# The activation of VectorE's channels, moved half a slot down in ScalarE's order (patch-matching denoiser, 8 images, one core)

## The chip, the cores and the metric

The kernel runs on one core of a Trainium2 chip. The core has TensorE (PE, matrix products), VectorE (DVE, elementwise work), ScalarE (ACT, activations and copies), GpSimd (POOL, here mostly an issuer of DMAs) and SyncE (SP, an issuer of DMAs). The metric is the device time in microseconds of the whole program. The profile is of one execution; all times in the views count from the start of its span.

## The reference

The input x has 8 images of 32 channels and 128 x 128 pixels, float32. Layer 0 normalises it by groups of channels (`_gn`), finds for each pixel the 8 of 25 neighbours in a 5 x 5 window whose 3 x 3 patches are nearest, and gathers them into 256 channels. These channels pass three stages, each a 1 x 1 convolution (256 to 256 channels) followed by a depthwise 3 x 3 convolution and an activation, and a final part:

```
dct = _conv(xb, dct_w, groups=C)
h = jax.nn.relu(_conv(_conv(xb, w1), w2, groups=CK, pad=1))
h = jax.nn.relu(_conv(_conv(h, w3), w4, groups=CK, pad=1))
wiener = jax.nn.sigmoid(_conv(_conv(h, w5), w6, groups=CK, pad=1))
filt = _conv(wiener * dct, inv_dct_w, groups=C)
return _conv(filt, agg_w)
```

x plus that result goes to layer 1, which normalises again and adds one 5 x 5 convolution per channel.

## The kernel before

An image is cut into strips of 8 rows, 16 and one partial strip per image, so 136 steps (`steps`) for 8 images; two more drain the pipeline. The main loop runs over steps, and inside a step over four slots, `for i in (3, 2, 1, 0)`: the slot of stage 3, of stage 2, of stage 1, and of the final part (0). Stage i works in step s on strip s - (i - 1), the final part on strip s - 2. So the result of stage 1 is read by stage 2 in the next step's slot 2, that of stage 2 by stage 3 in the next step's slot 3, and that of stage 3 by the final part in slot 0 of the step after: three slots after the one in which it was begun, each time.

The 256 channels are two halves of 128. For one half the depthwise convolution runs on TensorE (`depthwise_t`, tile pw, L751, activated out of PSUM by L764). For the other half it runs on VectorE (`depthwise_v`): the 1 x 1 convolution's result pv (L670) is copied to tile tv by ScalarE (L678, two copies), ScalarE writes the first tap into acc (L722), VectorE adds eight taps (L725, some 10.5 us), ScalarE applies the activation in place (L729), and SP copies two rows of tv for the next strip (`rows_before_v`, L655). The 1 x 1 convolution for the TensorE half is p (L694), copied to tile t by ScalarE (L701, two copies) and shifted between partitions by SP's DMAs (L707, L709, L648). Where the 1 x 1 convolution sums over both halves, pv takes four matmuls from acc[0], TensorE's half, and then four from acc[1], VectorE's half, and this twice (rows 0 to 3 and 4 to 7).

Beside the stages each slot selects and gathers one unit of neighbours for a later strip: a DMA by POOL brings indices (ib, L602), ScalarE turns them into one-hot selections (L616 and L617, twice a slot: `gather_select(..., (0,))` early and `(1,)` late), TensorE multiplies (pg, L631, 48 records) and ScalarE copies the result (L638). The next image's preparation (squared differences L444 and L452, sums pd L459, the choice of neighbours L536 and L537, transpositions), layer 1 (L897, L924, L936) and the final part (pc L810, the products L818, pa L831, L839) fill in from queues "D", "A", "P" and "Q" or at fixed places.

PE, DVE and ACT run in the order in which the program writes their instructions (`tc.manual_schedule`); the order of DMA issues on POOL and SP is set when the program is built. Generators hold back pieces of a stage for a later slot. `depthwise_v` writes L722 up to its first yield, the taps up to its second, the activation up to its third and then the row copy. In the main loop `new_v` is the generator begun in this slot, `dv` that of the slot before and `kept` that of the slot before that. `next(dv)` therefore writes the activation late in the slot after the taps, behind the queue "A" and ahead of the second selection, and `next(kept)` writes the row copy in the middle of the slot after that, behind `pointwise_t` and ahead of `gather_pixels`. The taps of stage 3 thus have their activation late in slot 2, those of stage 2 late in slot 1, those of stage 1 late in slot 0.

Of the kernel before, what the change touches and what calls it, by code (L numbers as in the profile page):

```python
# [44 lines left out]
def bm3d_conv_preact(  # L45
# [165 lines left out]
    def push(task):  # L211
        want = next(task, None)
        if want:
            which, cost, *wait = want
            queues[which].append((cost, task, now[0] + (wait[0] if wait else 0)))
# [54 lines left out]
    def weights():  # L270

        natural, kc = {}, None
        for i, (name, w) in enumerate((("w1", w1), ("w3", w3), ("w5", w5))):
            t = accp.tile([P, 2, R * W // 2], F32, name=f"nat_{name}", tag=f"acc{i + 1}0")
            natural[name] = t = t[:, :, :CK]
            nc.sync.dma_start(t, w.rearrange("(m p) i a b -> p m (i a b)", p=P))
        yield "D", 1.0, 8

        nat = natural["w1"]
        kc = accp.tile([P, 2, R * W // 2], F32, name="w1_kc", tag="acc31")  # L280
        natural["w1"] = kc = kc[:, :, :CK]
        for m in range(2):
            for g in range(2):
                nc.vector.tensor_copy(
                    kc[:, m, P * g : P * (g + 1)].rearrange("p (j c) -> p j c", c=C),
                    nat[:, m].rearrange("p (c j g) -> p g j c", j=4, g=2)[:, g],
                )
        for name, dst in (("w1", lw1), ("w3", lw3), ("w5", lw5)):
            for g in range(2):
                yield "P", 0  # L290
                ps = ps_x.tile([P, 512], F32, name=f"ps_{name}_{g}", tag="x")
                for m in range(2):
                    nc.tensor.transpose(
                        ps[:, m * P : (m + 1) * P],
                        natural[name][:, m, g * P : (g + 1) * P],
                        ident,
                    )
                nc.scalar.copy(dst[:, g], ps[:, :CK])
# [67 lines left out]
    def prep(b):  # L366

        xn = load_image(b, nc.gpsimd) if b else first
        yield "P", 0
        yield "D", 5.5  # L370
        st = work.tile([P, 8, 6], F32, name=f"st_{b}", tag="st")
        for i in range(8):
            nc.vector.bn_stats(
                st[:, i], xn[:, 3 + 4 * i : 7 + 4 * i, 2 : 2 + W]
            )
        mv = work.tile([P, 2], F32, name=f"mv_{b}", tag="mv")
        nc.vector.bn_aggr(mv, st.rearrange("p a b -> p (a b)"))
        yield "A", 0
        nc.scalar.copy(xn[:, :, 0:2], xn[:, :, 2:3].to_broadcast([P, HR, 2]))
        nc.scalar.copy(  # L380
            xn[:, :, 2 + W :], xn[:, :, 1 + W : 2 + W].to_broadcast([P, HR, 2])
        )
        mr = yield from group_stats(mv, f"a{b}")
        nc.vector.tensor_scalar(
            xn, xn, mr[:, 0:1], mr[:, 1:2], op0=ALU.subtract, op1=ALU.mult
        )
        push(sources(b, xn))

        idx = work.tile([P, 4, 8, K, 4], U32, name=f"idx_{b}", tag="idx", bufs=1)

        sq = dram.tile([NO // 2, 4, HR - 2, HX], F32, name=f"sq_{b}", tag="sq")
        for i in range((HR - 2) // SR):
            pd = ps_d.tile([P, SR // 2, HX], F32, name=f"pd_{b}_{i}", tag="pd")

            for aa in ((2, 4), (0, 0), (1, 1), (3, 2), (4, 3), (5, 5)):
                yield "D", PAIR
                push(squares(b, i, pd, xn, aa, sq, idx))
# [254 lines left out]
    def rows_before_v(i, b, n):  # L652
        v = tv[i - 1]
        if n < NS:
            nc.sync.dma_start(v[:, 0:2], v[:, R : R + 2])  # L655
        else:
            nc.gpsimd.memset(v[:, 0 : i + 1], 0.0)
# [53 lines left out]
    def depthwise_v(i, b, n):  # L711
        v = tv[i - 1]
        nr = R if n < NS else i
        out_ = accp.tile([P, R, W], F32, name=f"acc{i}_{b}_{n}_1", tag=f"acc{i}1")
        acc = out_[:, :nr]
        for k, (dy, dx) in enumerate(
            ((1, 1), (0, 0), (0, 1), (0, 2), (1, 0), (1, 2), (2, 0), (2, 1), (2, 2))
        ):
            tap = dwv[:, i - 1, 3 * dy + dx : 3 * dy + dx + 1]
            rows = v[:, dy : dy + nr, dx : dx + W]  # L720
            if k == 0:
                nc.scalar.activation(acc, rows, AF.Copy, scale=tap)  # L722
                yield out_
            else:
                nc.vector.scalar_tensor_tensor(  # L725
                    acc, rows, tap, acc, op0=ALU.mult, op1=ALU.add
                )
        yield
        nc.scalar.activation(acc, acc, funcs[i - 1])  # L729
        yield  # L730
        rows_before_v(i, b, n)

    def depthwise_t(i, b, n):
# [297 lines left out]
    def until(cond, credit):  # L1031
        while not cond():
            turn(credit)

    with tc.manual_schedule(engines=ORDERED):
        push(prep(0))
        push(weights())
        push(mixes())
        xbd[0] = dram.tile([P, 2, H, W], F32, name="xbd_0", tag="xbd")
        for i in range(3):  # L1040
            nc.gpsimd.memset(tb[i][0:64, 0], 0.0)
        for u in range(7):
            unit(gather_load, u)

            for _ in range({2: 3, 3: 1}.get(u, 0)):
                turn(4.0)
            unit(gather_select, u - 2)
            unit(gather_pixels, u - 3)
        u = 4

        dt = dv = kept = iter(())

        later = iter(())

        for s in range(len(steps) + 2):
            if s < len(steps):
                b, n = steps[s]
                if s == 2:
                    push(bands())
                if n == (0 if b else 4) and b + 1 < NB:  # L1060
                    until(lambda: b in ready, 4.0)
                    push(prep(b + 1))
                if n == NS - 1 and b + 1 < NB:
                    until(lambda: b + 1 in ready, 4.0)
                    xbd[b + 1] = dram.tile([P, 2, H, W], F32, name=f"xbd_{b+1}", tag="xbd")
            for i in (3, 2, 1, 0):
                si = s - (i - 1 if i else 2)
                live = 0 <= si < len(steps)
                new_v = new_t = iter(())
                if live:  # L1070
                    bi, ni = steps[si]

                if live and i:
                    src = source(i, bi, ni)
                    pointwise_v(i, bi, ni, lws[i - 1], src)
                    new_v, new_t = depthwise_v(i, bi, ni), depthwise_t(i, bi, ni)
                    accs[i, bi, ni] = [None, next(new_v)]
                next(later, None)
                if live and not i:
                    if ni == 0:  # L1080
                        x1d[bi] = dram.tile([C, H, W], F32, name=f"x1d_{bi}", tag="x1d")
                        stats[bi] = work.tile([P, NS + 1, 6], F32, name=f"stat_{bi}", tag="stat")
                    xr, xf, j0, j1 = fins.pop(si)
                run("P")
                if live and not i:
                    final_dct(bi, ni, accs[3, bi, ni], xf, j0, j1)

                run("Q")
                if s < len(steps):
                    unit(gather_select, u + 1, (0,))  # L1090
                    unit(gather_load, u + 3)
                    tick(b, i)
                next(later, None)
                next(new_v, None)
                if live and i:
                    pointwise_t(i, bi, ni, lws[i - 1], src)
                next(kept, None)
                if s < len(steps):
                    unit(gather_pixels, u)
                next(dt, None)  # L1100
                run("A")
                next(dv, None)
                if s < len(steps):
                    unit(gather_select, u + 1, (1,))
                    u += 1
                next(dt, None)
                kept, dv, dt = dv, new_v, new_t
                if live and not i:
                    later = end(bi, ni, xr, j0, j1)
                if not i and 0 <= s - 1 < len(steps):  # L1110
                    fins[s - 1] = final_load(*steps[s - 1])
        next(kept, None)
        for _ in later:
            pass
        until(lambda: {(NB - 1, 0), (NB - 1, 1)} <= done, 4.0)
# [62 lines left out]
```

## Time and profile before

| what | us |
|---|---|
| median of three runs (lowest, highest) | 6544.47 (6539.76, 6554.23) |
| the profiled execution's own time | 6544.27 |
| its span, first to last instruction | 6542.5 |
| granted TensorE clock, mean over the span | 0.98 |
| L725, VectorE's taps: busy, mean of one | 4032.1, 1.237 |
| L729, the activation: 408 times, busy, mean of one | 417.3, 1.023 |
| ScalarE idle just before L729, ended by VectorE's taps | 348.8 |

The main views are the page (busy time of each engine, the chain of work that ended last), the list of waits (who waited for whom, how much in total, how often, the longest), the timeline (start, duration, engine, line, operation, operands, count, and in brackets the idle time before and who ended it), and a table of stretches (from:to, length, busy time and number of instructions of each engine, granted clock, DMA share, GB/s). [...] A matmul record's duration overlaps with that of its neighbours, so lengths of groups are read from start to start.

### The profile page before, as it was taken

Reading aid. Unit: us, or ns where it says so; the run is one execution under the profiler, and the core shown is the slowest. Engines: PE = TensorE matmul, PEld = TensorE weight load, DVE = VectorE, ACT = ScalarE, POOL = GpSimd, SP = SyncE. Lnnn points to the kernel's source line nnn. Section 1 sums busy time; section 2 is a strip of 40 time slices with the busy share of each in tenths; the row PEclk is TensorE's granted clock in tenths of the full one; section 3 lists DMA queues with packets and bytes.
Section 4 is the critical chain, followed back from the end, with each engine's and each line's share of the span. In section 5 each row is a group of like instructions: output and inputs, shape, how many; then the busy total and the mean of one; then the engine's idle time right before and its main releaser. Section 6 shows DMA issues by size and latency. Waiting matters only on the chain.

```text
span 6542.5 us, 234200 instructions
## 1 busy us (share of the span) xinstructions
PE 6179.8 (94%) x102306; PEld 3215.9 (49%) x102306; DVE 5857.8 (90%) x8828; ACT 5058.6 (77%) x6698; POOL 3087.2 (47%) x5015
## 2 busy tenths in 40 slices
PE   4799999999999999999999999999999999999997
PEld 1444445455554545545454544544545454455553
DVE  7899988999989999999989999889998999878776
ACT  5787769778787877887788787977869788787772
POOL 8345436444364444644446444554345544334334
PEclk8899999999999999999999999999999999999998
DMA  4555555555555555565556555555555555455553
GB/s 85 126 134 144 125 126 143 141 143 138 131 149 138 137 146 129 145 151 134 140 132 156 136 137 141 134 142 140 139 135 134 146 146 138 115 147 144 136 134 81
DMA packets 544960, 886.21 MB, mean 135 GB/s; under 512 B 248880, under 2 KB 312944, under 8 KB 543936
## 3 DMA queue, kind: packets, MB, share of 16 engines
q0 software_dynamic: 383648, 611.87, 37.3%
q1 hardware_dynamic: 157776, 258.11, 16.1%
q8 instruction: 805, 13.19, 0.9%
q10 hardware_dynamic: 2512, 1.25, 0.1%
q14 instruction: 219, 1.79, 0.1%
HBM read 420.60 MB, written 216.49 MB: 97 GB/s over the span
## 4 chain that ended last, share of the span: by engine, by line
PE 55%; DVE 26%; POOL 5%; ACT 5%; DMA 4%; issue 4%; SPq 0%; ACTq 0%; DVEq 0%; POOLq 0%
PE pw L751 18%; DVE acc L725 17%; PE pv L670 14%; PE p L694 13%; PE pg L631 4%; POOL xtd L424 3%; DVE idx L537 3%; PE pc L810 2%; DMA t<-t 2%; DVE df L444 1%; PE pd L459 1%; PE p L924 1%; PE pa L831 1%; DVE acc L818 1%; ACT df L452 1%
## 5 line engine op out<-in xcount | busy, mean ns | idle before, releaser
L725 DVE SCALAR_TENSOR_TENSOR acc<-tv,dwv,acc 128x1024 f32<-128x1024 f32 (+3 forms) x3264 | 4032.1, 1237 | 163.7 <-ACT acc L722 59.9
L751 PE MATMUL pw<-t,dwd 96*32 96x254 f32 (+7 forms) x31680 | 2113.2, 419 | 23.8 <-DMA t<-t 17.9
L751 PEld LDWEIGHTS pw<-t,dwd 96*32 96x32 f32 (+1 forms) x31680 | 1079.9, 110 | 850.1 <-issue 385.5
L616 ACT ACTIVATE sel<-ib,nplace 128x1024 f32<-128x1024 uint8 x1024 | 1170.6, 1143 | 62.3 <-DMA ib<-idxd 62.3
L617 ACT ACTIVATE sel<-sel 128x1024 f32<-128x1024 f32 x1024 | 1086.0, 1061 | 32.5
L670 PE MATMUL pv<-acc,lw 128*32 128x512 f32 x8448 | 964.3, 593 | 49.9 <-DVE acc L818 41.7
L694 PE MATMUL p<-acc,lw 128*32 128x256 f32 x16768 | 977.4, 380 | 19.4 <-DVE xy L936 19.4
L602 POOL DMA_DIRECT2D ib<-idxd x512 | 293.0, 572 | 1209.2 <-ACT sel L616 1099.4
L791 POOL DMA_DIRECT2D xf<-xbd x1088 | 653.6, 633 | 329.2 <-PE pc L810 187.1
L694 PEld LDWEIGHTS p<-acc,lw 128*32 128x32 f32 x16768 | 568.0, 111 | 411.2 <-issue 59.3
L678 ACT COPY tv<-pv 128x512 f32<-128x512 f32 (+2 forms) x784 | 437.0, 578 | 366.9 <-PE pv L670 358.8
L729 ACT ACTIVATE acc<-acc 128x1024 f32<-128x1024 f32 (+3 forms) x408 | 417.3, 1023 | 349.0 <-DVE acc L725 348.8
L631 PE MATMUL pg<-sel,xt 120*32 120x88 f32 (+1 forms) x24576 | 609.9, 245 | 56.6 <-ACT sel L617 56.2
L631 PEld LDWEIGHTS pg<-sel,xt 120*32 120x32 f32 x24576 | 559.3, 111 | 211.5 <-ACT sel L617 72.2
L670 PEld LDWEIGHTS pv<-acc,lw 128*32 128x32 f32 x8448 | 289.1, 111 | 531.8 <-issue 414.6
L764 ACT ACTIVATE acc<-pw 128x512 f32<-128x512 f32 (+2 forms) x808 | 438.7, 573 | 143.6 <-PE pw L751 141.0
L444 DVE TENSOR_TENSOR df<-xn 128x786 f32<-128x786 f32 (+2 forms) x576 | 530.5, 973 | 1.0 <-PE pd L459 0.7
L701 ACT COPY t<-p 128x512 f32<-128x512 f32 x800 | 423.9, 572 | 137.5 <-PE p L694 137.5
L452 ACT ACTIVATE df<-df 128x786 f32<-128x786 f32 (+2 forms) x576 | 457.8, 859 | 40.8 <-DVE df L444 39.5
L722 ACT ACTIVATE acc<-tv,dwv 128x1024 f32<-128x1024 f32 (+3 forms) x408 | 455.1, 1115 | 44.1 <-PE pa L831 29.7
L694 PE MATMUL p<-xb,lw 128*32 128x256 f32 x8192 | 473.5, 383 | 14.4 <-DVE xy L936 14.4
L844 POOL DMA_DIRECT2D x1d<-xr x544 | 278.3, 518 | 417.9 <-DVE xr L839 300.8
(155 smaller groups left out, 6053.2 us busy)
## 6 DMA issues: line engine op xcount, KB each, us to landing
ib<-idxd POOLq DMA_DIRECT2D x512, 256.0 KB, 4.1
xbd<-xb POOLq DMA_DIRECT2D x128, 1024.0 KB, 6.0
xf<-xbd POOLq DMA_DIRECT2D x960, 128.0 KB, 6.8
t<-t SPq DMA_DIRECT2D x792, 128.0 KB
t<-t SPq DMA_DIRECT2D x384, 256.0 KB
tv<-tv SPq DMA_DIRECT2D x384, 130.0 KB
xt<-xtd POOLq DMA_DIRECT2D x240, 180.0 KB, 3.9
xtd<-xl POOLq DMA_DIRECT2D x192, 96.0 KB, 3.3
```

The lines of the kernel that those rows point to most:

```text
L444: nc.vector.tensor_sub(df[:, :, ca:cz], xn[:, r0 : r0 + SR, ca:cz], xn[:, r0 + dy : r0 + dy + SR, ca + dx : cz + dx],)
L452: nc.scalar.activation(df[:, :, ca:cz], df[:, :, ca:cz], AF.Square)
L616: nc.scalar.activation(sel, ib, AF.Square, bias=nplace)
L617: nc.scalar.activation(sel, sel, AF.Relu, scale=-1.0, bias=1.0)
L631: nc.tensor.matmul(pg[C * j : C * (j + 1), :, :, xa:xz], xt[: 8 * QW, f * (NT // 2) + t], sels[j // 2][: 8 * QW, j % 2 * 2 : j % 2 * 2 + 2 ...
L670: nc.tensor.matmul(ps[C * j : C * (j + 1), :hr], lhsT[:, g, P + C * j : P + C * (j + 1)], src(g)[:, h : h + hr], start=g == 0, stop=g == 1,)
L694: nc.tensor.matmul(ps[C * r : C * (r + 1), e, :nb], lhsT[:, g, s], rows[:, r : r + 4 * nb - 3 : 4], start=g == 0, stop=g == 1,)
L722: nc.scalar.activation(acc, rows, AF.Copy, scale=tap)
L725: nc.vector.scalar_tensor_tensor(acc, rows, tap, acc, op0=ALU.mult, op1=ALU.add)
L751: nc.tensor.matmul(pt[u][C * j : C * (j + 1), ka:kz, :nb, xa:xz], dwd[0:hi, i - 1, u, j, dx + 1], t[0:hi, j, ka:kz, :nb, xa + dx : xz + dx ...
L764: nc.scalar.activation(rows[:, u : u + 2 * nh[u] - 1 : 2, :nb], pt[u][:, : nh[u], :nb], funcs[i - 1])
L791: nc.gpsimd.dma_start(xf[p : p + C, m, j0:j1], src[g, m, (h + m + 1) % 2, :, :, ya:yz])
```

## The change

The second of the three yields in `depthwise_v` that lie behind the taps goes, so the activation and the row copy are written together. The loop's names shift by one: what was begun in this slot is `new_v`, what was begun in the slot before is `made` and is left alone, and what was begun two slots before is `dv`, whose `next` now stands where `next(kept)` stood, behind `pointwise_t` and ahead of `gather_pixels`. The row copy keeps its place in the program; the activation moves from late in the slot after its taps to the middle of the slot after that. ScalarE's instructions in the middle of a slot become: the two copies L701, the activation of two slots before, the copy L638, queue "A", the second selection, the two activations L764.

```
--- before.py
+++ after.py
@@ -727,7 +727,6 @@
                 )
         yield
         nc.scalar.activation(acc, acc, funcs[i - 1])
-        yield
         rows_before_v(i, b, n)
 
     def depthwise_t(i, b, n):
@@ -1048,7 +1047,7 @@
             unit(gather_pixels, u - 3)
         u = 4
 
-        dt = dv = kept = iter(())
+        dt = dv = made = iter(())
...
@@ -1094,22 +1093,20 @@
                 next(new_v, None)
                 if live and i:
                     pointwise_t(i, bi, ni, lws[i - 1], src)
-                next(kept, None)
+                next(dv, None)
                 if s < len(steps):
                     unit(gather_pixels, u)
                 next(dt, None)
                 run("A")
-                next(dv, None)
                 if s < len(steps):
                     unit(gather_select, u + 1, (1,))
                     u += 1
                 next(dt, None)
-                kept, dv, dt = dv, new_v, new_t
+                dv, made, dt = made, new_v, new_t
...
-        next(kept, None)
         for _ in later:
             pass
```

## The prediction

> **What bounds the kernel now.** I read the page's busy shares and chain first, then the list of waits, then the timeline of one step, because the change moves one instruction in ScalarE's order and only the order's neighbours can pay for it.
>
> ```profile
> PE 6179.8 (94%) x102306; PEld 3215.9 (49%) x102306; DVE 5857.8 (90%) x8828; ACT 5058.6 (77%) x6698; POOL 3087.2 (47%) x5015
> ...
> PE 55%; DVE 26%; POOL 5%; ACT 5%; DMA 4%; issue 4%; SPq 0%; ACTq 0%; DVEq 0%; POOLq 0%
> ```
>
> TensorE (PE) is busy 6179.8 us and holds 55% of the chain. Its matmuls are the same before and after, so the time can fall only by what PE idles, 6542.5 - 6179.8 = 362.7 us; 115.9 of them lie in the first 250 us and 44.9 in the last 102.5 (busy times by stretches). ScalarE (ACT) carries 5% of the chain.
>
> ```profile
>   ACT acc L729: 348.8, 143
> ```
>
> That line, from the view of the taps L725, is what the change attacks: 143 of 408 times ACT stands at L729 until VectorE (DVE) has done its taps. Who is hurt by it is seen in PE's own waits (us, times, longest), here from 250 to 6470 us:
>
> ```profile
> PE pg L631 <- ACT sel L617: 47.0, 28, 2.2
> PE pv L670 <- DVE acc L818: 41.7, 20, 3.7
> PE p L694 <- DVE xy L936: 33.7, 18, 3.6
> PE pi L569 <- DVE oc L560: 20.6, 9, 8.6
> ...
> PE pc L810 <- ACT t L701: 13.9, 7, 3.4
> ```
>
> ACT's 348.8 us cost PE at most the 47.0 us at pg; the other large ones are DVE's own lateness, and the 13.9 us come from a late transfer (ACT's L616 waits 6 to 8 us for ib just before). So the prize is small.
>
> **The change, part by part.** A step has four slots, for stages 3, 2, 1 and the final one (0). Before, stage 3's activation stands late in slot 2, stage 2's late in slot 1, stage 1's late in slot 0, each ahead of the second selection (L616, L617) and of L764. After, they stand in slots 1, 0 and the next step's slot 3, behind the two copies L701 and ahead of the copy L638. PE's and DVE's orders do not change; no instruction is added. The readers are fixed: stage 2's and 3's pv (L670, from the fifth of its sixteen matmuls on) at the head of slots 2 and 3, and the products L818 in slot 0.
>
> *Readers in slots 3 and 0: nothing.* Between L701 and stage 3's pv, PE has pg and pw to do in slot 0, and pw alone takes some 5.2 us; DVE reaches L818 after 10.5 us of taps. An activation of 1.06 us fits; without that cover it would cost up to 1.06 us a step.
>
> *Reader in slot 2: a new stall.* Slot 3 has no pw, because the final stage has no depthwise part. Its end in one step:
>
> ```profile
> 3000.45 0.59 ACT L678 COPY tv<-pv 128x512 f32<-128x512 f32 x1 [1.13 <-PE pv L670]
> ...
> 3001.04 3.66 PE L694 MATMUL p<-acc,lw 128*32 128x256 f32 x64
> ...
> 3001.36 1.15 ACT L722 ACTIVATE acc<-tv,dwv 128x1024 f32<-128x1024 f32 x1 [0.33 <-PE pa L831]
> ...
> 3002.42 1.13 ACT L616 ACTIVATE sel<-ib,nplace 128x1024 f32<-128x1024 uint8 x1
> ...
> 3003.58 1.06 ACT L617 ACTIVATE sel<-sel 128x1024 f32<-128x1024 f32 x1
> ...
> 3004.50 1.15 PE L631 MATMUL pg<-sel,xt 120*32 120x88 f32 x48
> 3004.55 1.06 ACT L701 COPY t<-p 128x512 f32<-128x512 f32 x2
> ...
> 3005.42 3.66 PE L670 MATMUL pv<-acc,lw 128*32 128x512 f32 x32
> ```
>
> The last line is stage 2's pv: 32 records for 16 matmuls, 3.44 us from its start to that of the next PE work (3008.86). The first eight read the other half of the channels and take 3.44 x 8/32 = 0.86 us, so PE needs the activated tile at 3005.42 + 0.86 = 3006.28. ACT ends the copies at 3005.61, starts its next instruction about 0.1 us before that end (as between 3003.58 + 1.06 and 3004.55), so L729 runs from 3005.52 to 3006.58, and PE resumes 0.05 us after ACT's end (L617 ending at 2635.12, pg resuming at 2635.17). PE stalls 3006.63 - 3006.28 = 0.35 us. ACT's chain starts from stage 3's own pv and has no idle in it but the wait for pa, so nothing that the change frees makes it earlier. Worked out in the same way for the 127 full steps that show all these rows: 85 stalls of about 0.31 (26.7 us), 21 of about 0.05, where other PE work stands in the slot (1.1 us), and 21 of about 0.56 (11.8 us): **+40 us**. Bounds: none where ACT were 0.35 us quicker, and 1.06 us a step, 135 us, where PE had no cover at all; I take the rows' own difference.
>
> *What hides part of it.* Where PE later waits for DVE anyway, and DVE has not idled in between, the stall is swallowed. Going through those waits and counting the one or two stalls since DVE's last idle (each at 0.31, no more than the wait): **-16 us**; bounds 0 and -40. The seven waits for ib swallow one stall each: -2 us.
>
> *ACT behind the moved instruction.* In slot 3 there was no L729, now there is. So L638, the squares L452, the second selection, the copies L678 and L722 of slot 2 come up to 1.06 us later, unless ACT idled there. pg in slot 2 has 2 us in hand, the pd matmuls lose under 2 us in total. The taps behind L722 matter: in 20 steps DVE was free just then and starts up to 0.9 us later, 18 us in sum. DVE usually has that slack; about half falls where it is the late one: **+9 us** (bounds 0 and 18).
>
> *What it gives.* In slots 2, 1 and 0 ACT is one activation ahead of before where it runs without pause. Of the recurring waits at pg, the 2.18 us one (2635.17; six images) shrinks by 1.05 and the 1.22 us one by 0.4, the latter by an image-end tile: **-8 us**; the others follow a wait of ACT for DMA or for another engine, after which ACT has one L729 ahead of the selection as before. At the end of the span, L764 stood behind an L729 that waited 5.85 us, and PE with it for 1.4 and 2.45 us; the taps then bind: -1 us (bounds 0 and -4).
>
> *The clock.* PE's idle can cost more than itself:
>
> ```profile
> 3088.76:3092.17 3.41, 3.26 (x16) 0.79 (x20) 3.27 (x16) 3.38 (x5) 0.58 (x1) 0.50 1.08 247
> 3092.17:3095.58 3.41, 3.41 (x52) 1.42 (x48) 3.27 (x15) 1.91 (x4) 0.00 (x0) 1.00 0.79 174
> ```
>
> The numbers ahead of the last two are the granted clock: after an idle of 2.20 us the clock was 0.50 for 3.41 us, which costs 1.7 us. Four of the six waits of 2.18 us were followed by such a stretch (1051 to 1054 us at 0.50; 3421.5 to 3424.9 at 1.00 was one of the two spared). Shrunk to 1.13 us they may lose it, at most -7 us; I take -4. Stalls of 0.3 us, spread 46 us apart, start no such stretch in these rows. (The Trainium skill, "TensorE: Matmul & The Clock Gate", section "Part 1: The HAM clock gate (the "warmup" mystery)", has the half clock follow at least one idle window of about 3.4 us. By that rule neither 0.3 nor 2.2 us would cool PE, the -4 falls away, and the sum would be four us higher; the 0.50 above after 2.20 us goes against it, and the row decides.)
>
> *The queues.* SP issues the tv row copy L655 ahead of a t row copy in 11 places, at image ends; 0.5 us an issue, up to 5 us, and the t rows are wanted slots later: I take 0. POOL moves one ib load per image behind four stores L938 (6.08 us): issued at 2774.5 instead of 2764.6, landing some 4 us later, first read by L616 at 2789.7. Covered by about 10 us; uncovered, up to 10 us an image.
>
> Sum: 40 - 16 - 2 + 9 - 8 - 1 - 4 = **+18 us**. The profiled execution took 6544.27 us (span 6542.5 and 1.8 around it), the median of the three runs 6544.47: forecast **6562 us**, slower by 0.3%. About 0.2%, 13 us, is what a measurement of this kernel can tell from no change.
>
> **Rivals.**
> *Cancelled.* The stall is there but DVE's and DMA's waits take nearly all of it: PE waits 115 us for DVE in the list's window, room enough for 40. For it: the waits recur in every image. Against: most stalls are followed by an idle DVE (it waits 284.8 us for pa). Without the 40 - 16 - 2 that survive, and half of DVE's +9: 6544 + 5, 6549 us; its range is 13 us either way.
>
> *Faster.* ACT, no longer held 348.8 us, runs ahead, and PE loses its waits for selections, 47.0 us, perhaps with five half-clock stretches, 8 us. It needs the chain L722 to L729 to end 0.35 us earlier than read; below a stall of about 0.1 us this rival decides. Taking half: 6544 - 28 = 6516 us. Against: 28 waits in all, most behind a DMA or a run of squares.
>
> *Much slower.* No stall is swallowed and all of DVE's 18 us count, with a dozen more half-clock stretches where DVE's waits grow past 2 us: 6544 + 40 + 18 - 9 + 20 = 6613 us. Against: DVE's waits shrink, not grow, by what PE is late.
>
> **How the numbers follow.** Forecast (stall partly swallowed) 0.45, its own range 6558 to 6592; cancelled 0.34; faster 0.13; much slower 0.08. Slower than 6557.6: 0.45 + 0.08 = 0.53; within 0.2%: 0.34; faster: 0.13. The range 6530 to 6596 leaves out most of the last two cases' far halves, some 0.17.
>
> **What would show it.** Right: PE waits at pv L670 for ACT L729, some 100 times, about 0.3 us each; ACT's wait at L729 for DVE under 100 us instead of 348.8; pg's waits for L617 near 35 us; the waits of pv for L818 smaller. Wrong: no wait of pv for L729 (the chain is shorter than read), waits at it above 0.6 us (ACT reaches L701 later than now), or ib loads that L616 waits for (POOL's new order bites).

## The result and the profile after

The new kernel takes 6576.67 us (median of six runs, 6568.91 to 6583.36) against 6542.99 us of the old one (six runs, 6536.31 to 6554.23): a ratio of 1.0053, 95% interval 1.0042 to 1.0065. It is slower, as forecast; the loss is 34 us where 18 were forecast. From line 731 on, the new kernel's line numbers are one lower than the old one's (pw is L750, the products L817, layer 1's addition L935); L729, L722, L701 and L670 are where they were.

The busy shares of the new kernel (page):

```profile
PE 6207.7 (94%) x102306; PEld 3172.8 (48%) x102306; DVE 5858.3 (89%) x8828; ACT 5053.3 (77%) x6698; POOL 3076.9 (47%) x5015
```

PE's busy time is 27.9 us more for the same 102306 records (a matmul of the program has two, as in the prediction's 32 for 16). So most of the loss is not idle time in the list: it is in records that became longer. The rows below show two things that lengthen them: a stall that lies within a group of matmuls, and a halved clock.

The view of the activation, new kernel. Above, who ended ACT's idle time before it (us, times); below, who waited for it:

```profile
  DVE acc L725: 1.9, 1
...
  PEld pv L670: 148.1, 144
  PE pv L670: 17.2, 27
```

ACT's 348.8 us of waiting are gone, as foretold, and pv now waits for L729: 144 times at the weight loads (PEld), where the waits sum to far more than the 44 us that PE loses by it (worked out below), and 27 times as visible PE idle.

PE's own waits, new kernel, 250 to 6470 us (us, times, longest):

```profile
PE pv L670 <- DVE acc L817: 43.0, 21, 3.4
PE p L694 <- DVE xy L935: 42.1, 18, 4.7
PE pg L631 <- ACT sel L617: 29.9, 29, 1.9
...
PE pw L750 <- DMA t<-t: 16.8, 10, 4.2
PE pv L670 <- ACT acc L729: 14.5, 24, 1.0
...
PE pd L459 <- ACT df L452: 7.4, 8, 1.1
```

Against the list shown of the old kernel, pg fell from 47.0 to 29.9, and p's wait for VectorE's xy rose from 33.7 to 42.1 with a longest of 4.7 instead of 3.6. No step of the prediction speaks of that last line. The same step as in the prediction, new kernel (timeline):

```profile
3021.19 1.14 PE L631 MATMUL pg<-sel,xt 120*32 120x88 f32 x48
3021.22 1.06 ACT L701 COPY t<-p 128x512 f32<-128x512 f32 x2
...
3022.14 3.93 PE L670 MATMUL pv<-acc,lw 128*32 128x512 f32 x32
3022.17 1.07 ACT L729 ACTIVATE acc<-acc 128x1024 f32<-128x1024 f32 x1
...
3023.13 0.59 ACT L638 COPY xb<-pg 128x512 f32<-128x512 f32 x1
...
3023.59 1.64 ACT L452 ACTIVATE df<-df 128x792 f32<-128x792 f32 x2
...
3025.89 0.85 PE L459 MATMUL pd<-df,neg 128*32 128x396 f32 x8
```

From pv's start to pd's start it is now 3.75 us, before 3.44: the stall is 0.31 us (0.35 was worked out). It appears as a longer pv (3.93 against 3.66), not as idle time. Summed from start to start over all steps, pv behind pg is 37 us longer in 119 steps (0.31 on average: 0.3 in 76 of them, 0.1 in 20) and pv behind p, at image ends, 10 us in 10; in seven steps, where pi waits for VectorE next, 3 us shorter. Together 44 us.

### What the forecast did not look at

Subtracting the old kernel's start-to-start times from the new one's, group by group, leaves one item that is not a stall at L729: in the step in which stage 2 works on strip 3, in six images, the stretch from pd to pg. Old kernel, timeline of the third of these places:

```profile
2764.38 0.87 PE L459 MATMUL pd<-df,neg 128*32 128x396 f32 x8
...
2765.04 1.93 PE L694 MATMUL p<-acc,lw 128*32 128x256 f32 x32
...
2767.43 1.27 DVE L936 TENSOR_TENSOR xy<-xy,p 128x512 f32<-128x512 f32 x2
...
2768.15 1.93 PE L694 MATMUL p<-acc,lw 128*32 128x256 f32 x32 [1.18 <-DVE xy L936]
...
2769.90 1.12 PE L631 MATMUL pg<-sel,xt 120*32 120x88 f32 x48
```

New kernel, the same place:

```profile
2770.57 0.85 PE L459 MATMUL pd<-df,neg 128*32 128x396 f32 x8
...
2775.36 1.27 DVE L935 TENSOR_TENSOR xy<-xy,p 128x512 f32<-128x512 f32 x2
...
2776.08 5.80 PE L694 MATMUL p<-acc,lw 128*32 128x256 f32 x64 [4.66 <-DVE xy L935]
...
2781.71 1.13 PE L631 MATMUL pg<-sel,xt 120*32 120x88 f32 x48
```

The two halves of stage 2's p (32 records each) are written to PSUM banks of the pool `ps_x`, five banks that pv, p, pg, pa, pc and layer 1's own p (L924) share. A bank that layer 1's p holds comes free only when VectorE has added it (L936). In the old kernel the second half of stage 2's p has such a bank; in the new one the first half has it, as the banks in the two built programs say. Nothing in the source names a bank: the pool hands them out when the program is built, and 1932 of its 3066 tiles lie in another bank than before, though PE's and VectorE's orders are the same instruction by instruction. So PE now stops 32 records earlier for the same event. And the longer idle halves the clock (columns: busy time of PE, PEld, DVE, ACT, POOL, then the granted clock):

```profile
2770.00:2776.00 6.00, 1.42 (x16) 0.26 (x8) 5.79 (x17) 5.91 (x7) 0.00 (x0) 0.80 0.34 88
2776.00:2784.00 8.00, 7.92 (x140) 4.54 (x144) 7.82 (x8) 2.59 (x5) 6.64 (x5) 0.72 0.24 38
```

The clock is 0.50 from 2773.64 to 2780.47; p takes 5.63 us instead of 3.45. From pd's start to pg's start the six places take 8.1 us on average in the old kernel and 10.9 in the new one, 17 us in sum.

### The profile page after: what moved, and what is told of

Its sections match the earlier page's. It is cut to its first block, busy times and chain, and to the rows that moved or that the text cites. A ratio compares the mean times of both kernels' runs of the same rounds, so it can differ in the third digit from the quotient of the medians.

```text
span 6574.3 us, 234367 instructions
## 1 busy us (share of the span) xinstructions
PE 6207.7 (94%) x102306; PEld 3172.8 (48%) x102306; DVE 5858.3 (89%) x8828; ACT 5053.3 (77%) x6698; POOL 3076.9 (47%) x5015
## 3 DMA queue, kind: packets, MB, share of 16 engines
q10 hardware_dynamic: 2512, 1.25, 0.1%
## 5 line engine op out<-in xcount | busy, mean ns | idle before, releaser
L750 PE MATMUL pw<-t,dwd 96*32 96x254 f32 (+7 forms) x31680 | 2112.7, 419 | 23.6 <-DMA t<-t 21.2
L750 PEld LDWEIGHTS pw<-t,dwd 96*32 96x32 f32 (+1 forms) x31680 | 1072.8, 110 | 854.5 <-issue 382.7
L616 ACT ACTIVATE sel<-ib,nplace 128x1024 f32<-128x1024 uint8 x1024 | 1177.3, 1150 | 59.8 <-DMA ib<-idxd 59.8
L670 PE MATMUL pv<-acc,lw 128*32 128x512 f32 x8448 | 985.3, 592 | 73.8 <-DVE acc L817 43.0
L694 PE MATMUL p<-acc,lw 128*32 128x256 f32 x16768 | 985.2, 383 | 29.9 <-DVE xy L935 29.9
L763 ACT ACTIVATE acc<-pw 128x512 f32<-128x512 f32 (+2 forms) x808 | 453.1, 577 | 395.7 <-PE pw L750 394.4
L670 PEld LDWEIGHTS pv<-acc,lw 128*32 128x32 f32 x8448 | 264.7, 110 | 600.8 <-issue 349.7
L701 ACT COPY t<-p 128x512 f32<-128x512 f32 x800 | 425.6, 572 | 150.5 <-PE p L694 150.5
L722 ACT ACTIVATE acc<-tv,dwv 128x1024 f32<-128x1024 f32 (+3 forms) x408 | 455.0, 1115 | 54.0 <-PE pa L830 42.1
L452 ACT ACTIVATE df<-df 128x786 f32<-128x786 f32 (+2 forms) x576 | 458.6, 865 | 41.3 <-DVE df L444 40.5
L670 PE MATMUL pv<-xb,lw 128*32 128x512 f32 x4096 | 466.3, 594 | 0.0
```

What stands on the lines that cost most here:

```text
L452: nc.scalar.activation(df[:, :, ca:cz], df[:, :, ca:cz], AF.Square)
L616: nc.scalar.activation(sel, ib, AF.Square, bias=nplace)
L670: nc.tensor.matmul(ps[C * j : C * (j + 1), :hr], lhsT[:, g, P + C * j : P + C * (j + 1)], src(g)[:, h : h + hr], start=g == 0, stop=g == 1,)
L694: nc.tensor.matmul(ps[C * r : C * (r + 1), e, :nb], lhsT[:, g, s], rows[:, r : r + 4 * nb - 3 : 4], start=g == 0, stop=g == 1,)
L750: nc.tensor.matmul(pt[u][C * j : C * (j + 1), ka:kz, :nb, xa:xz], dwd[0:hi, i - 1, u, j, dx + 1], t[0:hi, j, ka:kz, :nb, xa + dx : xz + dx ...
L763: nc.scalar.activation(rows[:, u : u + 2 * nh[u] - 1 : 2, :nb], pt[u][:, : nh[u], :nb], funcs[i - 1])
```

## The experiments

The theories that the expectations name: A, two causes that add up, the stall of pv and the bank; B, the stall alone, the bank's wait being swallowed by later waits; C, ScalarE's other instructions, which come later in slot 3 by one activation. Ratios are to the old kernel, run on the same chip. "kept" and the three yields are the old kernel's, where the diff is against it.

### Which part of the change costs

Against the old kernel, stages 3 and 2 moved, stage 1 not:

```
                     pointwise_t(i, bi, ni, lws[i - 1], src)
+                if i != 3:
+                    next(kept, None)
                 next(kept, None)
...
-                next(dv, None)
+                if not i:
+                    next(dv, None)
...
```

> Stage 1's activation goes back to its old place, late in slot 0; those of stages 3 and 2 stay half a slot later. The new kernel is 33.7 us slower than the old one. Theory A, two causes: the stall of stage 2's pv at L729 (about 0.3 us in each of some 125 steps), and the order in which PSUM banks are handed out, which changed between the two builds: once an image p L694 now gets the bank of layer 1's p one tile earlier and waits 4.7 us for VectorE's xy instead of 1.2. This kernel has the new kernel's banks and no stall, so 10 to 20 us slower than the old one, with no wait of pv for L729 and with the waits of 4.7 us. Theory B, the stall alone, the bank order swallowed by later waits: 15 us faster to equal. Theory C, ScalarE's other instructions, later by one activation in slot 3: equal within 8 us.

Measured: 1.0011 (1.0003 to 1.0020), +7 us, 6552.77 us. That is below A's range, above B's and within C's. Stage 1's move is worth most of the loss, and something is left without any stall. p's waits for xy are long here, as in the new kernel (45.7 us, longest 5.1), which speaks against C but shows nothing by itself.

Against the old kernel, stage 1 alone moved (`if i == 3:` in place of `if i != 3:`, and `if i:` in place of `if not i:`):

> Only stage 1's activation is moved, those of stages 3 and 2 are where they were. In this build p L694 has the old kernel's bank at the disputed place. Theory A: the stall without the bank's cost, 10 to 22 us slower than the old kernel, pv's waits for L729 as many as in the new one (some 140 at PEld), p's wait for xy near 1.2 us. Theory B: 30 to 45 us slower, since it keeps the stall and loses what the earlier pg gained. Theory C: about 30 us slower as well, told from B by the next kernel.

Measured: 1.0035 (1.0023 to 1.0048), +23 us. This lies just above A's range and below B's (the interval is 15 to 31 us); less than the whole loss, with the stall there as often as expected (136 waits of pv's weight loads) and p's waits for xy at 30.2 us, speaks for A but doesn't settle it.

### The bank, put back and taken alone

Against the old kernel, all moved but stage 2's activation of strip 2 (8 of 408 instructions):

```
+            undo = 0 < s <= len(steps) and steps[s - 1][1] == 2
             for i in (3, 2, 1, 0):
...
+                if i in (3, 1) or (i == 0 and not undo):
+                    next(kept, None)
                 next(kept, None)
...
-                next(dv, None)
+                if i == 1 and undo:
+                    next(dv, None)
```

> The new kernel, but in one step of each image (strip 2 of stage 2, 8 of 408 activations) the activation stays at its old place. That alone gives p L694 its old bank at the disputed place. Theory A: 12 to 22 us faster than the new kernel, so 12 to 22 us slower than the old one, with p's wait for xy back near 1 us and pv's waits for L729 unchanged. Theories B and C: as the new kernel, 30 to 35 us slower than the old one, 8 moved activations being worth under 3 us.

Measured: 1.0021 (1.0012 to 1.0030), +14 us, as A has it; 21 us faster than the new kernel, for eight instructions. The timeline at the place:

```profile
2772.54 0.85 PE L459 MATMUL pd<-df,neg 128*32 128x396 f32 x8
2773.20 1.91 PE L694 MATMUL p<-acc,lw 128*32 128x256 f32 x32
2775.59 1.93 PE L694 MATMUL p<-acc,lw 128*32 128x256 f32 x32 [0.47 <-DVE xy L936]
```

The first half runs at once again. The counter-test is the old kernel with only those eight activations moved:

```
+            alone = 0 < s <= len(steps) and steps[s - 1][1] == 2
...
+                if i == 0 and alone:
+                    next(kept, None)
                 next(kept, None)
...
-                next(dv, None)
+                if not (i == 1 and alone):
+                    next(dv, None)
```

> The old kernel, but in one step of each image (strip 2 of stage 2, 8 of 408 activations) the activation is written half a slot later. No stall of pv at L729 comes of that; p L694 gets the new kernel's bank at the disputed place. If the bank is a cause by itself: 12 to 20 us slower than the old kernel, with p's wait for xy 4 to 5 us there and VectorE's wait for L722 up from 31 to about 46 us between 250 and 5700 us. If it costs only together with the moved activations: within 5 us.

Measured: 1.0032 (1.0019 to 1.0046), +21 us (12 to 30), without one of the other 400 activations moved and without a stall at L729. The timeline at the place:

```profile
2771.03 0.85 PE L459 MATMUL pd<-df,neg 128*32 128x396 f32 x8
2777.03 6.28 PE L694 MATMUL p<-acc,lw 128*32 128x256 f32 x64 [5.16 <-DVE xy L936]
```

PE's waits of this kernel, from 250 to 6470 us:

```profile
PE p L694 <- DVE xy L936: 47.7, 18, 5.6
```

At the six places the stretch from pd to pg is 8.1 us on average in the old kernel and 11.4 here: 20 us in sum, the measured loss. (Either edit shuffles other banks too; that the loss equals what these six places lose is why it is put down to them.) The eight moved activations by themselves gain: PE's waits at pg are 40.8 us here, 47.0 in the old kernel. So the 21 us are what the bank costs less that gain. VectorE pays too, since p's lateness makes the next tile's L722 late. Its waits at the taps from 250 to 5700 us, the old kernel and then the new one:

```profile
DVE acc L725 <- ACT acc L722: 31.2, 69, 2.5
```

```profile
DVE acc L725 <- ACT acc L722: 46.7, 71, 2.9
```

With the bank put back this wait is 30.4 us, with the bank alone 42.8, and with stages 3 and 2 moved 46.9: it goes with the bank, not with the stall.

### The stall, taken away by two roads and lengthened

First road, against the new kernel: stage 2's pv sums TensorE's half of the channels for both halves of the rows and only then VectorE's half.

```
-            ps = ps_x.tile([P, 4, W], F32, name=f"pv{i}_{b}_{n}_{h}", tag="x")
-            for g in range(2):
-                for j in range(4):
...
+        for g, h in (
+            [(g, h) for g in range(2) for h in hs]
+            if i == 2
+            else [(g, h) for h in hs for g in range(2)]
+        ):
...
+            ps = pss[h // 4]
+            for j in range(4):
...
```

> The new kernel with one edit: stage 2's pv sums TensorE's half of the channels for both halves of the rows first, and only then VectorE's half, so that the activated tile is needed 1.72 us after pv's start instead of 0.86. The stall of 0.3 us must vanish, while ScalarE's order and the banks stay those of the new kernel. Theory A: 10 to 22 us slower than the old kernel (the banks' part is left). Theory B: equal, within 10 us. Theory C (later instructions of ScalarE): as the new kernel, 30 us slower.

Measured: 1.0038 (1.0025 to 1.0052), +25 us (16 to 34): only some 10 us better than the new kernel, and the two intervals overlap. The stall itself is gone (pv is line 677 here; 3.44 us from its start to pd's):

```profile
3016.10 3.63 PE L677 MATMUL pv<-acc,lw 128*32 128x512 f32 x32
3019.54 0.86 PE L459 MATMUL pd<-df,neg 128*32 128x396 f32 x8
```

That rules out B. A wanted a little less and C no gain at all; the interval reaches both, so this kernel doesn't tell them apart. The same edit with the old bank:

> The new kernel with the old bank at the disputed place and with the other order of sums in stage 2's pv, so neither the bank's wait nor the stall is left; ScalarE's order stays that of the new kernel but for one activation an image. If stall and bank make the loss: within 5 us of the old kernel, or faster. If ScalarE's later instructions in slot 3 cost by themselves (the sums' order alone was worth only 8 us): 6 to 12 us slower than the old kernel.

Measured: 1.0000 (0.9991 to 1.0009), equal to the old kernel. Between these two kernels the bank is worth some 25 us. What stages 3 and 2 gain was still to be measured. Stages 3 and 2 moved, without the stall and with the old bank (`i == 1` in place of `i in (3, 1)`, and `i == 0 or (i == 1 and undo)` for the late place):

> Stage 1's activation at its old place (no stall) and, in one step of each image, stage 2's too (the old bank); the rest of stages 2 and 3 half a slot later. Two causes that add up: 8 to 18 us faster than the old kernel (stage 1 back was worth 25 us and the bank 20 us of the 34 lost). If the two overlap, because each is taken back by the same waits for VectorE: within 6 us of the old kernel.

Measured: 0.9969 (0.9956 to 0.9982), 20 us faster than the old kernel, 6525.05 us. That is just past the 8 to 18 us of two causes that add up, which lie within the interval (12 to 29). By the point values stage 1's activation in slot 3, with its stall taken away by the order of sums, still costs 20 us. To tell ScalarE's load from a cost of that order, the second road: in slot 3 stage 1's activation is written ahead of the copies L701.

```
                 next(new_v, None)
+                if i == 3:
+                    next(kept, None)
                 if live and i:
                     pointwise_t(i, bi, ni, lws[i - 1], src)
...
```

> The new kernel with the old bank at the disputed place, and with stage 1's activation in slot 3 written ahead of the two copies L701 instead of behind them. It then ends before pv needs it, so the stall is gone by another road than the order of sums, and ScalarE still has one instruction more in slot 3 ahead of L638, the squares L452 and the second selection. If that load is what costs the 20 us between the kernel with the other order of sums (equal to the old one) and the one with stage 1 at its old place (20 us faster): within 6 us of the old kernel. If the other order of sums had a cost of its own: 12 to 25 us faster than the old kernel.

Measured: 0.9983 (0.9973 to 0.9993), 11 us faster than the old kernel, between the two expectations. By this road ScalarE's load costs 9 us (from -20 to -11), but the intervals of the two kernels overlap, and L701 too comes one activation later here; so the 9 us are not clear of noise and not of one cause. The other order of sums, or L729's place behind L701, costs 11 more; why, these runs don't say. With the new kernel's bank:

> The new kernel with one edit: stage 1's activation in slot 3 is written ahead of the copies L701, so that the stall of pv is gone; the bank at the disputed place stays the new kernel's, with p's wait for xy of 4 to 5 us. If the terms add up (stall 25, bank 20, later ScalarE 9, gain -20): 9 us slower than the old kernel, 3 to 15. If the stall is worth only the 8 us that the other order of sums gave: 20 to 30 us slower.

Measured: 1.0009 (1.0000 to 1.0017), +6 us, where the sum of the terms has 9. By the second road the stall is worth 25 us (from -11 to +14, old bank) or 29 (from +6 to +35, new bank), by the first 10 to 14.

Against the new kernel, stage 1's activation one instruction further down:

```
-                next(dv, None)
+                if i != 3:
+                    next(dv, None)
                 if s < len(steps):
                     unit(gather_pixels, u)
+                if i == 3:
+                    next(dv, None)
```

> The new kernel, with stage 1's activation written one instruction further down in slot 3, behind the copy L638. It then ends some 0.7 us later, and pv's stall grows from 0.3 to about 1.0 us a step in some 115 steps, 80 us more in sum. If stalls reach the end of the span in full: 70 to 80 us slower than the new kernel. If the waits for VectorE swallow them in all images but the last, as the traces of the new kernel and of the one with the other order of sums say: 10 to 25 us slower than the new kernel, most of it after 5700 us.

Measured: 1.0099 (1.0082 to 1.0117), +65 us, 30 more than the new kernel. The pv behind pg is 85 us longer in the same 119 steps, 0.72 each, and now shows as idle time (250 to 6470 us):

```profile
PE pv L670 <- ACT acc L729: 110.1, 135, 1.4
```

So about a third of what PE is later there reaches the end; the 30 us lie above the 10 to 25 of the second case and far below the 70 to 80 of the first. Where the rest goes can be read from the two profiles, between 250 and 6470 us: PE's waits for VectorE sum to 86 us here and to 116 in the new kernel, and the clock stands at 0.50 for 92 us here and for 157 there, up to 32 us of matmul time. The expectation that most of it would be found after 5700 us was wrong: of the 27 us by which PE's last group starts later than in the new kernel's profile, 19 were there at 2855 us and 25 at 5676.

### Where the gain is

Only stage 2 moved, but for strip 2:

> Only stage 2's activation is moved, but for one step of each image (the old bank stays); stages 3 and 1 are as in the old kernel. The gain of 20 us seen with stages 3 and 2 moved should be stage 2's: once an image pg L631 waits 2.18 us for a selection that stood behind stage 2's activation, late in slot 1, and the clock halves after it. If so: 12 to 20 us faster than the old kernel. If stage 3's part counts as much: 6 to 12 us faster.

Measured: 0.9970 (0.9960 to 0.9981), 20 us faster than the old kernel, 6523.02 us. Only stage 3 moved:

> Only stage 3's activation is moved, from late in slot 2 to the middle of slot 1. The banks at the disputed place are the old kernel's. If the gain is stage 2's: within 5 us of the old kernel. If both count: 6 to 12 us faster.

Measured: 0.9994 (0.9986 to 1.0003), no difference. The gain is stage 2's. It lies at pg in slot 0, whose second selection ScalarE writes late in slot 1, until now behind stage 2's activation. The old kernel's wait there and the same wait here (timelines):

```profile
2635.17 1.06 PE L631 MATMUL pg<-sel,xt 120*32 120x88 f32 x41 [2.18 <-ACT sel L617]
```

```profile
2624.67 1.00 PE L631 MATMUL pg<-sel,xt 120*32 120x88 f32 x40 [1.20 <-ACT sel L617]
```

PE's waits at pg fall from 47.0 to 31.4 us, and the four half-clock stretches behind the six waits of 2.18 us are gone. This kernel, with nothing but stage 2's activation moved and one strip left out, is faster than both kernels.

## Why the prediction was right in sign and low in size

Measured, the parts are: stages 3 and 2 moved -20, ScalarE later in slot 3 +9, the stall +25, the bank +20; together +34 (each difference is good to some 8 us or more). The forecast's sum had -13, +9, +22 and nothing. That the parts come to the measured +35 is no proof: they are differences along one chain of kernels, from the old one to the new one, and must add up to it. What tests them are kernels outside the chain. The bank alone cost 21 us. Stage 1 ahead of L701 with the new bank was to cost 9 and cost 6; stages 3 and 2 with the new bank were to cost about 1 and cost 7. But stage 1 alone was to cost 25 + 9 = 34 and cost 23 (15 to 31), which stays unexplained. The forecast's own terms, without the bank, are best held against the kernel with the bank put back: +14 us, where 18 were forecast. So the sign is no luck. That the two come so close partly is: the gain was taken 7 us too small and the stall 3 or more, and these errors cancel.

- **"PE's and DVE's orders do not change"** was true and taken for too much. This is the step that failed: from the same order it was concluded that nothing changes but ScalarE's timing, so who shares a PSUM bank with whom was never looked at. The runs showed 17 to 27 us in its place (21 both by putting it back and by doing it alone). It was there to be read before any run, in the semaphores that p's two halves wait for in the two built programs: PE then VectorE in the old one, VectorE then PE in the new one.
- **The new stall, +40.** Right in place, count and size: 0.31 us a step, 44 us in sum instead of 40, of which 10 are at image ends where pv follows p. "What hides part of it", -16 and -2, left 22; the second road gives 25 to 29, the lengthened stall a survival of a third. The first road gives 10 to 14, and that difference is open. One sign of the forecast failed: pv's waits for L818 didn't shrink (41.7 us, then 43.0). With equal banks, though, all of PE's waits for VectorE between 250 and 6470 us are 10 us (old bank) and 11 us (new bank) less in the profiles with the stall than in those with stage 1 ahead of L701, where 16 were taken.
- **ACT behind the moved instruction, +9.** 9 by the second road, not clear of noise, and not only by VectorE's taps: pd waits for L452 7.4 us in the new kernel (1.8 before), where under 2 were allowed.
- **What it gives, -8 and -1.** Right in place (pg, once an image), low in size: pg's waits fell by 17.1 us, from 47.0 to 29.9 (near 35 was foretold). The six waits of 2.18 us fell to 1.27, much as forecast. The six of 1.22 us (2591.21 in the old kernel) did not shrink by 0.4 but grew to 1.85: ahead of that selection ScalarE is now rid of stage 2's activation and has stage 3's instead (0.9 with stage 2 alone moved, 2.16 with stage 3 alone). More than made up for it: six waits of 2.22 us (2739.34) fell to between 0.6 and 1.3, and six of 1.0 us to 0.2, which the forecast left as they were. At the end of the span pw's two waits for L764 (3.9 us) are gone.
- **The clock, -4.** Right at the place that it was taken from: the four half-clock stretches behind the waits of 2.18 us are gone. Wrong in sign for the whole kernel: between 250 and 6470 us the clock stands at 0.50 for 126 us in the old kernel, 157 in the new one, 147 with the bank alone and 120 with the bank put back. Behind pg's waits there are three such stretches instead of seven, all at waits that grew to 1.85 us, but p's longer waits bring more. 31 us at 0.50 are up to 15 us of matmuls, so a good part of the bank's price is paid in clock.
- **The queues, 0.** L616's waits for ib are 59.8 us in the new kernel and 62.3 in the old one: right.
- **The rivals.** Cancelled: the swallowing exists, but two thirds at most, and the bank is outside it; its sum is also wrong as it stands, since +18 without the 22 and half of the 9 is -8.5, 6536 us and not 6549. Faster: its mechanism, pg released by a ScalarE that runs ahead, is real and worth the 20 us of stage 2; it lost to the stall in slot 2, as the forecast said, and to the bank, as it didn't. Much slower: its 6613 us were not reached; its half-clock stretches came, for another reason.

## What to carry to other kernels

Equal instruction orders on the bound engine do not mean equal waits: where a pool hands out PSUM banks or buffers when the program is built, compare what each matmul waits for in the two builds, and look up which reader frees the bank that each tile gets. Move each stage's instruction by itself before judging a change that moves three of them: here one of the three holds all the gain and another all of the stall. A stall of a few tenths of a microsecond hides in the length of a matmul group, so read such groups from start to start.

## What was unexpected of the hardware

An idle PE of less than 2 us was enough to halve the clock. In the kernel with the other order of sums, pg ends an idle of 1.84 us at 2595.39, and the clock is 0.50 from 2596.20 to 2599.61; pw, 5.17 us long at the same place in the kernel with stages 3 and 2 moved, takes 6.84. Timeline:

```profile
2595.39 1.06 PE L631 MATMUL pg<-sel,xt 120*32 120x88 f32 x40 [1.84 <-ACT sel L617]
```

Busy time by stretch (the clock, third from the end, is a mean over four microseconds):

```profile
2596.00:2600.00 4.00, 4.00 (x67) 3.65 (x60) 3.96 (x6) 3.94 (x6) 3.25 (x6) 0.57 0.54 124
```

The Trainium skill, "TensorE: Matmul & The Clock Gate", section "Part 1: The HAM clock gate (the "warmup" mystery)", asks for an idle window of about 3.4 us: the 4.66 us at p agree with it, the 1.84 us here do not. An idle of 1.25 us at pg (stages 3 and 2 moved, old bank, 2625.97) was followed by a pw of 5.16 us at full clock. The length of one idle doesn't decide, though: with stages 3 and 2 moved and the new bank, pg ends an idle of 1.85 us at the same place (2595.12), and the clock stays full. In the fourteen profiles of this document the clock changes only at borders 3.41 us apart. Between 250 and 6440 us, PE had idled for 1.4 us or more in the 3.41 us before each of the 454 borders at which it fell from 1.00 to 0.50, and for 2.1 us at most before the 24384 at which it stayed at 1.00. By these counts it is the idle between two borders that matters: all of the 1.84 us above, but only 1.63 of the 1.85, the rest of which lies ahead of a border. So a wait of about two microseconds costs PE up to 1.7 us beyond itself, where it doesn't fall across a border, and a change that shortens it to 1.2 can gain both.
